# A spectral-and-attention kernel: both halves of a picture in one transfer, eight direct key steps, and a reordered tail

## The chip, the cores and the metric

The kernel runs on one core of one Trainium2 chip. The metric is the device time of one execution in microseconds. The text names the engines as the profile does: PE (TensorE), DVE (VectorE), ACT (ScalarE), POOL (GpSimd) and SP (SyncE). SP, ACT and POOL also issue DMA transfers, each from its own queue, in program order.

## The reference

Four pictures of 64 channels and 96 x 96 pixels pass through two residual layers, each behind a group normalization with 32 groups. The first layer is attention over all 9216 pixels with a sigmoid in place of a softmax, followed by a channel gate. The second multiplies the 16 lowest modes along the width and 32 along the height of a 2-D Fourier transform by complex 64 x 64 matrices.

```python
def reference(x, wq, bq, wk, bk, wv, bv, ca_w1, ca_w2, W_pos_re, W_pos_im, W_neg_re, W_neg_im):
    # layer 0, u = gn(x)
    q, k, v = conv1x1(u)                       # 8, 8 and 64 channels
    att = sigmoid(einsum('bcn,bcm->bnm', Q, K))
    out = einsum('bcm,bnm->bcn', V, att) + u
    scale = sigmoid(mlp(out.mean) + mlp(out.max))
    x = x + out * scale
    # layer 1, u = gn(x)
    u_hat = rfft2(u)
    top = einsum('bchw,cohw->bohw', u_hat[:, :, :16, :16], W_pos)
    bot = einsum('bchw,cohw->bohw', u_hat[:, :, -16:, :16], W_neg)
    return x + irfft2(top and bot put back, zeros elsewhere)
```

## The kernel before

**Layout.** A picture lies in SBUF on 128 partitions of 4608 elements (`HALF`): the upper half of the picture (48 rows of pixels) with its 64 channels on partitions 0 to 63, the lower half on 64 to 127. In DRAM a picture is [64 channels][9216]. `xf` and `outf` are views of it as [half e][channel c][4608]. `read` and `write` (lines 97 to 103) move columns of a picture in two transfers of 64 rows, one for each half, each on a queue that the caller gives. `read` is used for the first loads of all four pictures, for `old` (the original picture, again, for the second layer of the first three), and for `again` (the same for the last one); `write` for the result. The loads of the first picture are nine chunks of 512 columns, with the halves on SP and ACT; the other three are three chunks of 1536 columns each, all on SP. SP also issues the two parts of the constants `cs`, one behind the first picture, one behind the fourth.

**Attention.** Queries go in 9 blocks of 512 (`NBLK`) for each picture. For a block there are 144 tiles of 128 keys by 512 queries; a key step holds eight tiles, so there are 18 steps (0 to 17). A planner ahead of the emission fixes bursts of up to seven tiles: PE makes the energies of burst t+1 (`energies`, L556), ACT their sigmoids (`sigmoids`, L577), and PE multiplies those of the burst before with the values (`attend`, L594). PE, ACT and DVE run in exactly that written order (`manual_schedule`). Other work is put between bursts: `together` beside a burst (in PSUM banks that it leaves free), `alone`, and `ends` behind it.

For the first picture keys are made beside the attention that uses them. A *direct* key step is a matmul into PSUM (`key_matmuls`, L441) and three DVE instructions (`key_splits`: L452, L453, L436) that write `kT`. `DIRECT` is the number of such steps. The others come with the values: `values_of` projects 512 pixels (L475); DVE takes `u` and the values (L492, L482), splits them into high and low parts (L510, L511) and transposes them (L513); SP sends the result to DRAM in `qk` (L517); POOL fetches it into `stage` with the rows repeated (`known_keys`, L526); and DVE copies it into `kT` (L528), two bursts after the fetch was written down for the first picture and six for the others. Queries of later blocks come back from `qk` through SP (`queries`, L534). In block s, `values_of` leaves the key part out while 2s is below `DIRECT`.

**Second layer of the first three pictures.** It runs hidden beside the attention of the next picture, in strips of 768 columns: `fetch` reads `old`, `result` forms the layer's input on DVE (L185) and stores it, `turned`, `along_w` and `along_h` are the transform, `mixing` and `back_h` go back to DRAM and return through `zd` (L384 loads `z` in four transfers for each call), and `back_w` loads the stored input, adds (L403) and writes the result.

**Tail.** The last picture's gate and second layer have nothing to hide behind. Around the gate, matmuls on the constants with no use for the result keep PE busy: two at L923 ahead of it, and `occupy(n, behind, pd, cols)` (L970), which issues n of them behind a given instruction. Then, strip by strip, DVE forms the input (strips 4 and 5 by ACT and an adding DMA of POOL), transposes it (L1001), and PE transforms along W into `pa`, in two groups of three strips (L1011). `rows_turned(n)` transposes one group (L1018); `rows(n)` transforms along H into `pu` (L1023). The statistics go by `steps`: `steps[3]` is the matmul at L170, DVE's `ve` (L172) and POOL's power (L173). The mixing is 256 small matmul records (L220), of which DVE and ACT take turns to move the result out (L135, L137). `keep` stores six of the eight groups of rows in DRAM (`vd`, L231), `back` loads them into `vt` with the modes on partitions (L242): 16 rows in four transfers, and 8 rows in four. The last two groups come by `picked`, a matmul that selects rows, and DVE adds them to `vt` (L1104). Then the inverse along H (`pz_last`, L1114), four transposes (L1122), the inverse along W (`py`, L1132), the addition to the picture (L1140), and the writes (L103) of half a strip twice and five strips.

Of the kernel before, what the change touches and what calls it, by code (L numbers as in the profile page):

```python
# [33 lines left out]
F32 = mybir.dt.float32  # L34
# [6 lines left out]
P = 128  # L41
B, C, H, W = 4, 64, 96, 96
# [5 lines left out]
KW = 16  # L48
# [6 lines left out]


SIZE, HEAD = 7, 4
DIRECT = 12
AHEAD = 6 * SIZE
ALL = B * NBLK * TILES  # L60
ENGINES = {mybir.EngineType.PE, mybir.EngineType.Activation, mybir.EngineType.DVE}
# [23 lines left out]
NGROUP = 2  # L85
NPICK = 2
PICK = C + 4 * (NPICK - 1)
LATE = {"fw": NSQ * P, "fh": NGROUP * 2 * P, "pick": SIDE * PICK, "gh": 2 * P}


@with_exitstack
def tile_kernel(ctx: ExitStack, tc: tile.TileContext, x, cst, late, spec, out):
# [1 line left out]
    xf = x.rearrange("b c (e h) w -> b e c (h w)", e=2)  # L94
    outf = out.rearrange("b c (e h) w -> b e c (h w)", e=2)

    def read(to, p, cols, queues):
        for e in range(2):
            queues[e].dma_start(to[bass.ts(e, C)], xf[p][e, :, cols])

    def write(p, cols, of, queues):
        for e in range(2):
            queues[e].dma_start(outf[p][e, :, cols], of[bass.ts(e, C)])  # L103

    const = ctx.enter_context(tc.tile_pool(name="const", bufs=1))
    xpool = ctx.enter_context(tc.tile_pool(name="xpool", bufs=1))
# [5 lines left out]
    for p in range(B):  # L112
        xt = xpool.tile([P, HALF], F32, tag=f"x{p}", name=f"x{p}")
        step = NB if p == 0 else 3 * NB
        for s in range(HALF // step):
            cols = bass.ts(s, step)
            read(xt[:, cols], p, cols, (nc.sync, nc.scalar if p == 0 else nc.sync))
        if p == 0:
            nc.sync.dma_start(cs[:, :NFIRST], cst[:, :NFIRST])
        xs.append(xt)  # L120
# [4 lines left out]
    def named(name, rows=P):  # L125
        return cs[:rows, PLACE[name]]
# [118 lines left out]
    class Hidden(Mixing):  # L245
# [14 lines left out]
        def fetch(self, p, s):  # L260
            self.olds[p, s] = self.work.tile([P, STRIP], F32, tag="old", bufs=2,
                                             name=f"old_{p}_{s}")
            read(self.olds[p, s], p, bass.ts(s, STRIP), (nc.sync, nc.sync))

        def result(self, p, s, gate):

# [121 lines left out]
        def back_w(self, p, s):  # L388


            cols = bass.ts(s, STRIP)
            old = self.work.tile([P, STRIP], F32, tag="old", bufs=2, name=f"x1_{p}_{s}")
            nc.sync.dma_start(old, self.x1d[p][:, cols])
            py = self.banks(2)
            for i in range(2):
                for r in range(2):
                    rows, at = bass.ts(r, C), bass.ts(r, 2 * W)
                    for e in range(2):
                        nc.tensor.matmul(py[bass.ts(e, C), r, bass.ts(i, 2 * W)],  # L399
                                         self.z[rows, H // 8 * e + 2 * s + i, p, :],  # L400
                                         named("gw")[rows, at], start=True, stop=True)
# [3 lines left out]
            write(p, cols, old, (nc.sync, nc.sync))  # L405

    with tc.tile_pool(name="work", bufs=1) as work, \
# [289 lines left out]
        def bring(s):  # L699

            if s == 0:
                again.append(xpool.tile([P, HALF], F32, tag="vT0", name="again"))
            cols = bass.ts(s, STRIP)
            read(again[0][:, cols], B - 1, cols, (nc.sync, nc.sync))

        chain, ready, started = [], [0], [0]

# [211 lines left out]
        spare[0] = 7  # L919
        gate, steps, f = after(B - 1)  # L920
        with tc.issue_after(attended[0].ins):
            for n in (NB, NB // 2):
                nc.tensor.matmul(banks[:, 3, :n], cs[:, :P], cs[:, :n], start=True, stop=True)  # L923
        for step in steps:
            step()
# [2 lines left out]
    with tc.tile_pool(name="tail", bufs=1, reuse_waits="tile") as tail, \  # L928
# [45 lines left out]
        l1 = Mixing(1, bank_m, evacuate)  # L974
        l1.wts = wts
        idle = small_bank.tile([P, NB], F32, tag="idle", name="idle")
        occupy(3, projected[0], idle)

        mr, steps, mv = group_stats(None, bank_m, "l1_last")
        less = small.tile([P, 1], F32, tag="less", name="less")  # L980
# [54 lines left out]
        with tc.manual_schedule(engines=ENGINES):  # L1035
            for s in range(NSTRIP):
                if s not in ADDED:
                    combine(p, s, gate, again[:, bass.ts(s, STRIP)])
                strip(s)
                if s in (1, 3):  # L1040
                    steps[s // 2]()
            var = small.tile([P, 1], F32, tag="var", name="var")
            rows_turned(0)
            rows(0)
            nc.vector.tensor_reduce(var, squares, AX.X, ALU.add)
            nc.vector.tensor_scalar(mv[:, 1:2], var, 1.0 / HALF, None, ALU.mult)
            steps[2]()
            steps[3]()
            rows_turned(1)
            rows(1)  # L1050
            nc.vector.tensor_scalar(less_constant, mr[:, 0:1], mr[:, 1:2], float(-H),
                                    ALU.mult, ALU.mult)
            nc.vector.transpose(t, pu.rearrange("q (c k) -> q k c", k=KW))
            for h in (slice(0, 8), slice(8, KH)):
                nc.scalar.activation(u[:, :, :, h, 0], turned[:, :, :, h], AF.Copy,
                                     scale=mr[:, 1:2])
                for to, of in ((lo, hi), (hi, lo)):
                    nc.vector.tensor_scalar(
                        u[to, :, :, h, 1], turned[of, :, :, h], mr[of, 1:2],
                        -1.0 if to == lo else 1.0, ALU.mult, ALU.mult)  # L1060
                if h.start == 0:
                    l1.constant_mode(0, less_constant)
# [16 lines left out]
        for q in range(KH // 4):  # L1079
            l1.mix(q, 0)  # L1080
            l1.mix(q, 1)
            if q <= last - NPICK:
                l1.keep(q, nc.sync)
            if q == 3:
                nc.gpsimd.memset(vt, 0.0)
            for first, rows_of, behind in ((0, 16, last - 1), (16, 16 - 4 * NPICK, last)):
                if q == behind:
                    with tc.issue_after(moved[1].ins):
                        for half in range(2):
                            for slot in range(2):  # L1090
# [11 lines left out]
                        picks[:, 2 * half + n, at:at + C], l1.vms[q][:, bass.ts(2 * half + n, M)],  # L1102
                        start=(q == last - NPICK + 1), stop=(q == last))
        nc.vector.tensor_tensor(vt, picked, vt, ALU.add)  # L1104
        occupy(1, l1.last, mix_bank.tile([P, NB], F32, tag="v", name="idle_v", bufs=6), NB // 2)

        banks.close()
        pz_bank, py_bank = psum("ps_z"), psum("ps_y", 2)
        pz = pz_bank.tile([P, 4, NB], F32, tag="z", name="pz_last")
        for i in range(2):  # L1110
            for e in range(2):
                for half in range(2):
                    rows_of = bass.ts(half, 2 * KH)
                    moved[0] = nc.tensor.matmul(  # L1114
                        pz[:, 2 * e + half, :].rearrange("q (k o) -> q k o", o=C)[
                            :, :, bass.ts(i, C // 2)],
                        gh[rows_of, e, :], vt[rows_of, :].rearrange("q (k o) -> q k o", o=C)[
                            :, :, bass.ts(i, C // 2)], start=True, stop=True)
        z = tail.tile([P, C, SQ], F32, tag="z", name="z_last")
        for i in range(4):  # L1120
            cols = bass.ts(i, C // 4)
            nc.vector.transpose(z[:, cols, :],  # L1122
                                pz.rearrange("q x (k o) -> q o (x k)", o=C)[:, cols, :])
        occupy(2, moved[0], py_bank.tile([P, 2, NB], F32, tag="y", name="idle_y")[:, 0])
        for s in range(NSTRIP):
            for part in ([0], [1]) if s == 0 else ([0, 1],):
                py = py_bank.tile([P, 2, NB], F32, tag="y", name=f"py_{s}_{part[0]}")
                for n, i in enumerate(part):
                    for r in range(2):
                        rows_of = bass.ts(r, C)  # L1130
                        for e in range(2):
                            nc.tensor.matmul(  # L1132
                                py[bass.ts(e, C), r, bass.ts(n, 2 * W)],
                                z[rows_of, :, H // 8 * e + 2 * s + i],
                                named("gw")[rows_of, bass.ts(r, 2 * W)], start=True, stop=True)
                n = len(part)
                cols = slice(s * STRIP + part[0] * STRIP // 2,
                             s * STRIP + (part[0] + n) * STRIP // 2)
                o = x1[:, cols].rearrange("q (i r m) -> q i r m", r=2, m=2 * W)
                nc.vector.tensor_tensor(  # L1140
                    o, py[:, :, :2 * W * n].rearrange("q r (i m) -> q i r m", i=n), o, ALU.add)
                write(p, cols, x1[:, cols], (nc.sync, nc.scalar))


def _constants(l0):
# [68 lines left out]
    fours = np.zeros((2 * KH, 2, 4, SQ))  # L1214
    fours[..., :H // 4] = np.concatenate(gh, 1).reshape(2 * KH, 2, H // 4, 4).transpose(0, 1, 3, 2)
    b.append(np.tile(fours.reshape(2 * KH, 2 * P), (2, 1)))
    return a, np.concatenate(b, 1).astype(np.float32)


# [28 lines left out]
```

## Time and profile before

| what | us |
|---|---|
| median of 3 runs (lowest, highest) | 3045.09 (3043.98, 3045.64) |
| the profiled execution | 3046.73 |
| its span, from the first to the last instruction | 3044.6 |
| PE busy | 3012.3 |
| ACT busy | 2406.3 |
| DVE busy | 338.1 |
| POOL busy | 135.2 |

The span leaves out what the device spends before the first and after the last instruction of the kernel, 2.1 us of the profiled execution. Busy times are sums over instructions; PE's end times are modelled, so a busy PE is not one at its peak. The granted clock of PE is 0.996 over the span. The page of the profile lists DMA queue 1 (SP), 10 (ACT) and 0 (POOL); a DMA packet is one row of a transfer, and some packets of four bytes come with each transfer beside its rows.

### The profile page before, as it was taken

What the parts mean: (1) busy time and instruction counts of PE and PEld (TensorE: products, weight loads), DVE (VectorE), ACT (ScalarE), POOL (GpSimd) and SP (SyncE); (2) the same over time, 40 slices, a digit from 0 to 9 for tenths busy, and PEclk for the clock granted to TensorE, in tenths of its full rate; (3) what the DMA queues carried; (4) which work ended last, traced back from release to release, by engine and by line L of the source; (5) the groups of instructions that cost most, each with busy time, mean ns of one, the idle gap of its engine ahead of it and who ended that gap; (6) DMA issues with size and microseconds to landing.
All of it is one profiled execution on the core that took longest, in us unless ns stands there. A gap on an engine that the chain in (4) does not pass through costs nothing.

```text
span 3044.6 us, 44711 instructions
## 1 busy us (share of the span) xinstructions
PE 3012.3 (99%) x19368; PEld 1097.0 (36%) x19368; DVE 338.1 (11%) x818; ACT 2406.3 (79%) x1539; POOL 135.2 (4%) x275
## 2 busy tenths in 40 slices
PE   7999999999999999999999999999999999999997
PEld 3333333333333333333333333333333333333334
DVE  3200000002211000001311000000221100000004
ACT  4788888887888888888788888888788777777782
POOL 0100000003100000001300000000310000000000
PEclk9999999999999999999999999999999999999999
DMA  6100000002230000000332000000244243312224
GB/s 153 23 4 4 4 4 4 4 1 46 75 80 17 4 4 4 4 4 21 73 78 72 4 4 4 4 4 2 44 108 98 91 141 88 53 51 69 60 85 152
DMA packets 156869, 133.00 MB, mean 44 GB/s; under 512 B 118752, under 2 KB 123040, under 8 KB 156384
## 3 DMA queue, kind: packets, MB, share of 16 engines
q1 hardware_dynamic: 144544, 108.85, 14.2%
q0 software_dynamic: 10704, 18.83, 2.1%
q8 instruction: 152, 2.49, 0.3%
q10 hardware_dynamic: 1424, 2.46, 0.3%
q14 instruction: 45, 0.37, 0.0%
HBM read 90.81 MB, written 38.47 MB: 42 GB/s over the span
## 4 chain that ended last, share of the span: by engine, by line
PE 97%; DMA 1%; issue 0%; DVE 0%; ACT 0%; SPq 0%; ACTq 0%; POOL 0%; DVEq 0%
PE banks L594 77%; PE banks L556 16%; DMA x<-in_x_dram 1%; PE banks L475 1%; PE banks L220 1%; PE banks L399 0%; PE pv L220 0%; PE banks L305 0%; ACT at L577 0%; PE pa L1011 0%; PE banks L371 0%; DMA qk<-turned 0%; PE banks L333 0%; PE idle L970 0%; PE banks L441 0%
## 5 line engine op out<-in xcount | busy, mean ns | idle before, releaser
L577 ACT ACTIVATE at<-banks 128x2048 f32<-128x2048 f32 (+1 forms) x1505 | 2388.6, 1638 | 563.9 <-PE banks L556 545.1
L594 PE MATMUL banks<-at,vT 128*64 128x512 f32 (+1 forms) x11780 | 2410.6, 549 | 0.0
L594 PEld LDWEIGHTS banks<-at,vT 128*64 128x64 f32 x11780 | 774.3, 136 | 1352.3 <-issue 1297.5
L556 PE MATMUL banks<-q,kT 32*128 32x512 f32 x5040 | 543.3, 453 | 0.6 <-ACT at L577 0.4
L556 PEld LDWEIGHTS banks<-q,kT 32*128 32x128 f32 x5040 | 224.0, 183 | 453.4 <-issue 330.1
L600 DVE SCALAR_TENSOR_TENSOR x<-banks,x 128x512 f32<-128x512 f32 x36 | 24.9, 691 | 1664.9 <-PE banks L594 1664.9
L526 POOL DMA_DIRECT2D stage<-qk x240 | 117.9, 499 | 959.1 <-DMA qk<-turned 951.4
L173 POOL TENSOR_TENSOR mr_l<-ve_l,cs 128x1 f32<-128x1 f32 x7 | 3.9, 556 | 1292.4 <-DVE ve_l L172 1292.4
L403 DVE TENSOR_TENSOR x<-banks,x 128x768 f32<-128x768 f32 x18 | 17.2, 958 | 212.5 <-PE banks L399 201.4
L475 PEld LDWEIGHTS banks<-cs,x 64*64 64x64 f32 x1152 | 22.8, 136 | 27.3 <-ACT at L577 25.3
L492 DVE TENSOR_TENSOR u<-banks,cs 128x128 f32<-128x128 f32 x35 | 10.2, 290 | 189.8 <-PE banks L475 189.8
L744 POOL DMA_DIRECT2D w_early<-in_spec_dram x12 | 6.4, 543 | 521.7 <-PE banks L399 357.5
L475 PE MATMUL banks<-cs,x 64*64 64x80 f32 (+1 forms) x1152 | 28.5, 237 | 0.0
L556 PE MATMUL banks<-q_first,kT 32*128 32x512 f32 x144 | 18.0, 463 | 9.8 <-DVE full_k L452 6.6
L482 DVE TENSOR_TENSOR vT<-banks,cs 128x256 f32<-128x256 f32 x72 | 26.9, 414 | 0.0
L720 DVE COPY ae<-banks 128x512 f32<-128x512 f32 x9 | 6.2, 692 | 174.8 <-PE banks L305 128.9
L602 DVE TENSOR_REDUCE maxs<-x 128x1 f32<-128x512 f32 x36 | 24.7, 686 | 1.2
L608 DVE BATCH_NORM_STATS2 stats<-x 128x6 f32<-128x512 f32 x36 | 23.4, 680 | 6.1 <-DMA x<-in_x_dram 6.0
L720 DVE COPY ws<-banks 128x512 f32<-128x512 f32 x16 | 11.1, 691 | 116.8 <-PE banks L220 116.8
L185 DVE SCALAR_TENSOR_TENSOR x<-x,gate,old 128x768 f32<-128x768 f32 x18 | 18.2, 1009 | 17.7 <-DMA old<-in_x_dram 17.7
L513 DVE STREAM_TRANSPOSE turned<-t 128x384 f32<-128x384 f32 (+1 forms) x35 | 19.2, 549 | 1.2
L273 DVE STREAM_TRANSPOSE old<-x 128x768 f32<-128x768 f32 x18 | 17.6, 978 | 0.6
(143 smaller groups left out, 411.8 us busy)
## 6 DMA issues: line engine op xcount, KB each, us to landing
ws<-in_spec_dram SPq DMA_DIRECT2D x32, 512.0 KB
q<-qk SPq DMA_DIRECT2D x280, 32.0 KB
out_dram<-x SPq DMA_DIRECT2D x41, 192.0 KB
stage<-qk POOLq DMA_DIRECT2D x240, 32.0 KB, 1.9
x<-in_x_dram SPq DMA_DIRECT2D x18, 384.0 KB
old<-in_x_dram SPq DMA_DIRECT2D x36, 192.0 KB
x1d<-x SPq DMA_DIRECT2D x18, 384.0 KB
xd<-old SPq DMA_DIRECT2D x18, 384.0 KB
```

The costliest lines, as they stand in the source:

```text
L185: nc.vector.scalar_tensor_tensor(xs[p][:, cols], xs[p][:, cols], gate, old, ALU.mult, ALU.add)
L220: self.last = nc.tensor.matmul(pv[bass.ts(g, 32), :].rearrange("q (n k o) -> q n k o", n=SIDE, o=C)[:, :, k, :], self.ut[:, at:at + 32], s ...
L475: projected[0] = nc.tensor.matmul(pp[bass.ts(e, P // 2), b, 2 * a + h, :width], src[rows, a, h, bass.ts(e, P // 2)], named("wv")[rows, :wi ...
L482: nc.vector.tensor_tensor(vTs[p % 2][:, 8 * s:8 * s + 8, :].rearrange("p (a h b) m -> p b a h m", h=2, b=2)[:, b], pp[:, b, :, :C].rearran ...
L513: nc.vector.transpose(turned[:, k:].rearrange("p k a (m h) -> p (k a) h m", h=2), t[:, k:].rearrange("p k a h m -> p (k a) h m").bitcast(F32))
L526: nc.gpsimd.dma_start(come[bass.ts(r, QK), :], split[p][s // 2][:, r // 2, bass.ts(s % 2, NB // 2)])
L556: nc.tensor.matmul(banks[:, bank_of(i), :], kT[r:r + 32, i % TILES // 8, i // 4 % 2, :], ask[i // TILES][r:r + 32, :], start=True, stop=True)
L577: nc.scalar.activation(at[:, of:of + n, :], banks[:, bank:bank + n, :], AF.Sigmoid)
L594: attended[0] = nc.tensor.matmul(acc[half, cols], vTs[n // NBLK % 2][:, j, :], at[:, place(2 * pair + b), cols], start=(j == 0), stop=(j = ...
L600: nc.vector.scalar_tensor_tensor(blk, acc, 1.0, blk, ALU.mult, ALU.add, accum_out=sums[p][:, m:m + 1])
L602: mark[0] = nc.vector.tensor_reduce(maxs[p][:, m:m + 1], blk, AX.X, ALU.max)
L608: each = [lambda s=s: nc.vector.bn_stats(stats[:, s, :], xs[p][:, bass.ts(s, NB)]) for s in range(NBLK)]
```

## The change

- `read` and `write` issue one transfer for both halves. Its side in SBUF has 128 partitions; its side in DRAM has the dimensions [2 halves][64 channels][columns]. All reads go by SP. Writes in the tail go by SP and ACT in turn, a whole transfer each.
- `DIRECT` is 8 instead of 12: key steps 8 to 11 of the first picture now come through `qk` and `stage`.
- In the gate the fillers of L923 are 512, 512 and 128 columns instead of 512 and 256; the three fillers of 512 columns on `idle` become one of 512 and one of 256, and stand behind the two on `pa`.
- `rows_turned(1)` stands ahead of `steps[3]`.
- The loads into `vt` are no longer tied to ACT's last copy. The first 16 rows are issued by POOL, written down at q = 4, the next 8 by SP, at q = 5.
- `pz_last` becomes two tiles of half the channels, each transposed behind its own matmuls; the filler ahead of it is 512 columns instead of 256; the constants `gw` for the last inverse come with `late`, in another order of rows.

```diff
-DIRECT = 12
+DIRECT = 8
...
-LATE = {"fw": NSQ * P, "fh": NGROUP * 2 * P, "pick": SIDE * PICK, "gh": 2 * P}
+LATE = {"fw": NSQ * P, "fh": NGROUP * 2 * P, "pick": SIDE * PICK, "gh": 2 * P, "gw": 4 * W}
...
-    def read(to, p, cols, queues):
-        for e in range(2):
-            queues[e].dma_start(to[bass.ts(e, C)], xf[p][e, :, cols])
-
-    def write(p, cols, of, queues):
-        for e in range(2):
-            queues[e].dma_start(outf[p][e, :, cols], of[bass.ts(e, C)])
+    def read(to, p, cols, queue):
+        queue.dma_start(to, xf[p][:, :, cols])
+
+    def write(p, cols, of, queue):
+        queue.dma_start(outf[p][:, :, cols], of)
...
-            read(xt[:, cols], p, cols, (nc.sync, nc.scalar if p == 0 else nc.sync))
+            read(xt[:, cols], p, cols, nc.sync)
...
-            for n in (NB, NB // 2):
+            for n in (NB, NB, NB // 4):
                 nc.tensor.matmul(banks[:, 3, :n], cs[:, :P], cs[:, :n], start=True, stop=True)
...
-        occupy(3, projected[0], idle)
...
             with tc.issue_after(projected[0].ins):
-                nc.tensor.matmul(along_w[n][:, 3 * NB // 2:], cs[:, :P], cs[:, :NB // 2],
-                                 start=True, stop=True)
+                filled = nc.tensor.matmul(along_w[n][:, 3 * NB // 2:], cs[:, :P], cs[:, :NB // 2],
+                                          start=True, stop=True)
+        occupy(1, filled, idle)
+        occupy(1, filled, idle, NB // 2)
...
             steps[2]()
+            rows_turned(1)
             steps[3]()
-            rows_turned(1)
             rows(1)
...
-            for first, rows_of, behind in ((0, 16, last - 1), (16, 16 - 4 * NPICK, last)):
+            for first, rows_of, behind, queue in ((0, 16, last - 3, nc.gpsimd),
+                                                  (16, 16 - 4 * NPICK, last - 2, nc.sync)):
                 if q == behind:
-                    with tc.issue_after(moved[1].ins):
-                        for half in range(2):
-                            for slot in range(2):
-                                l1.back(vt, 64 * half + 32 * slot, first, rows_of, 0, slot,
-                                        2 * half, 2, (nc.scalar, nc.sync)[slot])
+                    for half in range(2):
+                        for slot in range(2):
+                            l1.back(vt, 64 * half + 32 * slot, first, rows_of, 0, slot,
+                                    2 * half, 2, queue)
...
-        occupy(1, l1.last, mix_bank.tile([P, NB], F32, tag="v", name="idle_v", bufs=6), NB // 2)
+        occupy(1, l1.last, mix_bank.tile([P, NB], F32, tag="v", name="idle_v", bufs=6))
...
-        pz = pz_bank.tile([P, 4, NB], F32, tag="z", name="pz_last")
+        z = tail.tile([P, C, SQ], F32, tag="z", name="z_last")
         for i in range(2):
+            pz = pz_bank.tile([P, 4, NB // 2], F32, tag=f"z{i}", name=f"pz_{i}")
             for e in range(2):
                 for half in range(2):
                     rows_of = bass.ts(half, 2 * KH)
                     moved[0] = nc.tensor.matmul(
-                        pz[:, 2 * e + half, :].rearrange("q (k o) -> q k o", o=C)[
-                            :, :, bass.ts(i, C // 2)],
-                        gh[rows_of, e, :], vt[rows_of, :].rearrange("q (k o) -> q k o", o=C)[
-                            :, :, bass.ts(i, C // 2)], start=True, stop=True)
-        z = tail.tile([P, C, SQ], F32, tag="z", name="z_last")
-        for i in range(4):
-            cols = bass.ts(i, C // 4)
-            nc.vector.transpose(z[:, cols, :],
-                                pz.rearrange("q x (k o) -> q o (x k)", o=C)[:, cols, :])
+                        pz[:, 2 * half + e, :], gh[rows_of, e, :],
+                        vt[rows_of, :].rearrange("q (k o) -> q k o", o=C)[:, :, bass.ts(i, C // 2)],
+                        start=True, stop=True)
+            for n in range(2):
+                cols = slice(i * C // 2 + n * C // 4, i * C // 2 + (n + 1) * C // 4)
+                nc.vector.transpose(z[:, cols, :], pz.rearrange(
+                    "q x (k o) -> q o (x k)", o=C // 2)[:, bass.ts(n, C // 4), :])
...
-                                named("gw")[rows_of, bass.ts(r, 2 * W)], start=True, stop=True)
+                                parts["gw"][rows_of, bass.ts(r, 2 * W)], start=True, stop=True)
...
-                write(p, cols, x1[:, cols], (nc.sync, nc.scalar))
+                write(p, cols, x1[:, cols], (nc.sync, nc.scalar)[(s + part[0]) % 2])
```

The other calls of `read` and `write` give SP's queue alone, as before. The scheduler sets `old` for the first two strips of the second layer early in SP's queue, before and after: nothing holds them back.

More of the change, by code (lines that the diff above doesn't have):

```diff
@@ L262, in fetch @@
                                              name=f"old_{p}_{s}")
-            read(self.olds[p, s], p, bass.ts(s, STRIP), (nc.sync, nc.sync))
+            read(self.olds[p, s], p, bass.ts(s, STRIP), nc.sync)
         def result(self, p, s, gate):
@@ L404, in back_w @@
                 o, py[:, :, :4 * W].rearrange("p r (i m) -> p i r m", i=2), o, ALU.add)
-            write(p, cols, old, (nc.sync, nc.sync))
+            write(p, cols, old, nc.sync)
     with tc.tile_pool(name="work", bufs=1) as work, \
@@ L703, in bring @@
             cols = bass.ts(s, STRIP)
-            read(again[0][:, cols], B - 1, cols, (nc.sync, nc.sync))
+            read(again[0][:, cols], B - 1, cols, nc.sync)
         chain, ready, started = [], [0], [0]
@@ L1216, in _constants @@
     b.append(np.tile(fours.reshape(2 * KH, 2 * P), (2, 1)))
+    by_half = np.arange(2 * KW).reshape(2, 2, KW // 2).transpose(1, 0, 2).ravel()
+    b.append(np.kron(np.eye(4), np.concatenate([twice * cw.T, -twice * sw.T], 0)[by_half]))
     return a, np.concatenate(b, 1).astype(np.float32)
```

## The prediction

> **What bounds the kernel now.** I read the page first: its busy shares, then the chain that ended last. The span is matmul throughput nearly everywhere.
>
> ```profile
> span 3044.6 us, 44711 instructions
> PE 3012.3 (99%) x19368; PEld 1097.0 (36%) x19368; DVE 338.1 (11%) x818; ACT 2406.3 (79%) x1539; POOL 135.2 (4%) x275
> ```
>
> PE is idle for only 32 us, so a change outside the attention loop gains at most that and what fillers take in the tail. It can lose far more: PE is in order, and it stops when keys are late. So the start comes next, in the chain of waits from 0 to 140 us (start, duration, what):
>
> ```profile
> 2.27 4.62 DMA x<-in_x_dram
> 6.91 4.00 DMA x<-in_x_dram
> ...
> 13.52 12.79 DMA x<-in_x_dram
> 26.33 14.79 DMA x<-in_x_dram
> 41.13 5.73 DMA qk<-turned
> ```
>
> All four pictures are loaded by 41 us, and until then the small transfers of queries and keys stand behind them on SP's queue. That costs one PE stall of 6.6 us. From the timeline of 40 to 130 us:
>
> ```profile
> 47.58 0.79 PE L556 MATMUL banks<-q_first,kT 32*128 32x512 f32 x1 [6.56 <-DVE full_k L452]
> ...
> 75.93 0.73 PE L556 MATMUL banks<-q_first,kT 32*128 32x512 f32 x7
> ...
> 92.20 4.14 POOL L526 DMA_DIRECT2D stage<-qk  x8 [75.17 <-DMA qk<-turned]
> ```
>
> The first burst of energies has 5 tiles, later ones 7; counting bursts, the one at 75.93 holds tiles 61 to 67, so the energy of tile 64, the first that needs key step 8 (8 tiles a step), runs at 76.0 us. The direct steps are 0 to 11 now, and the first keys that come back from DRAM arrive at 96 to 98 us, in time.
>
> Then the DMA side, in stretches (share of 16 DMA engines and GB/s are the last two columns):
>
> ```profile
> 33.00:41.00 8.00, 8.00 (x102) 3.58 (x101) 3.20 (x10) 3.79 (x3) 0.00 (x0) 1.00 1.02 234
> 2904.00:2914.00 10.00, 10.00 (x61) 3.38 (x57) 0.00 (x0) 9.04 (x6) 2.65 (x5) 1.00 1.02 409
> 3025.40:3029.20 3.80, 3.72 (x17) 3.31 (x18) 0.02 (x1) 0.00 (x0) 0.00 (x0) 0.55 0.00 0
> ```
>
> With 64 rows at a time the picture loads reach 234 GB/s with all 16 engines busy; 128-row weights reach 409, or 25.6 bytes a ns for each engine. In the tail (third line) the matmuls of pz run at a granted clock of 0.55.
>
> **How many engines a transfer gets.** The DMA view of 2622.9 to 2630 us holds just four ws<-zd transfers (L384), each of 8 outer by 24 inner rows:
>
> ```profile
> DMA  0003245576775665766566656676666655523310
> ...
> DMA packets 800, 0.39 MB, mean 55 GB/s; under 512 B 32, under 2 KB 800, under 8 KB 800
> ```
>
> The data are 4 x 192 = 768 packets, so 32 are left, 8 for each transfer, and the share stands at 5 to 7 tenths. A transfer of 64 rows leaves 16: ACT's nine x loads make 720 = 9 x (64 + 16) packets in the first 60 us. I read the small packets as one for each engine that takes part (the slices agree: 8 of 16 busy), so 192 rows behind an outer dimension of 8 had 8 engines, not 16. The changed transfers have two halves outermost in DRAM.
>
> [...] By it every read and write of a picture runs on two engines, and the sum is a large loss. [...] no row here shows an outer 2. [...]
>
> **The change part by part.** The sum is made against the profiled execution (3046.7 us, of which 2.1 lie around the span); it is 1.6 above the median of the runs, 3045.1.
>
> *Loads on two engines.* Each of the two moves half of each picture: 4 x 64 rows x 18,432 B = 4.72 MB, at 25.6 B/ns 184 us. From 2.1 us that is 186, and their eight rows each of the two constants transfers (2452 + 3472 B) add 2: 188. The rate is unknown for two engines alone; the nearest bounds are 25.6 and 234/16 = 14.6. I take the upper, since two engines ask for 51 GB/s of a path that gives 234; the lower would put the loads at 325 us.
>
> *Eight direct steps.* Step 8 now goes u, turned (L513), qk (SP), stage (POOL), kT (DVE). On SP's queue the qk transfers stand behind all loads, and a share of each lies on the two slow engines. After 188: the end of the second qk set, q_1, the third set, q_1 again: 13 issues of 0.42 us and one landing of 2, 195.5. Next in SP's order stand two old loads for the second layer, which nothing holds back so early: 2 x 64 x 3072 B / 25.6 = 15.4 us on the two engines, 211. Then qk of block 4 (0.9, and 1.2 to land) 213; four stage issues of 0.5 (499 ns on the page) and 1.9 to land, 217; the copy (0.24), 217.4. PE would be at tile 64 by about 107 us, although the last chunk of picture 0 comes 38 us later (nine chunks of 64 x 2048 B / 25.6 take 46 us, not 9): 76 + 38 less the old stall. So PE waits from there to 217.4, against 76.0 before: **+141.4**. ACT and DVE queue behind the same wait (the kT copy stands ahead of u of block 6). Keys 9 to 17 then follow at 2 us each and are wanted at 3.8 to 4.6: nothing. Four key steps leave PE; three of them lay after tile 64: 3 x 0.63 = **-1.9**. The removed stall of 6.6 us is inside the difference.
>
> *Old, again and out in the second layer.* Each old or out takes 7.7 us plus landing, where it took about 2. Old is covered by the 23 us between strips (six bursts of 3.8, which is 0.66 of L556 and 3.16 of L594 in the chain), except where DVE already waited 6.75 us for it (third strip of each hidden picture); there 5 us more, under attention that needs DVE only at block ends. The outs of the first three pictures come every 12 us and SP has 3 us of q loads in 80: covered; if not, back_w would hold a bank. I put **+3** for all.
>
> *The gate and along-W.* Gate fillers go from 768 to 1152 columns, 2.3 us for 1.56: they end at 2982.4, when f arrives: 0, costing their excess if f were earlier. Behind the gate 1280 filler columns stand ahead of pa in place of 2048; L970's 1536 took 4.54 us at a low clock. PE lags the strips there, so pa ends about 1.4 earlier. The row turn of group 1 (L1018, 1.24) moves ahead of ve (L172): it no longer waits for pv, while ve and POOL's pow wait for it, but both are done 1 us before pu. rows(1) follows at once instead of 1.4 after: together the mixing starts **-2.9** earlier.
>
> *Modes back.* The vt loads stood behind ACT's last copy (3018.5) and landed at 3024.5. Now 16 rows go by POOL once q 0 to 3 have landed (4 x 0.5 + 1.9, beside the mixing) and 8 rows by SP behind the last vd (3017.0, landing 1.8; four issues of 0.3, landing 1.5): 3021.6. The sum into vt starts **-3.0**. No POOL work waits behind its loads.
>
> *pz and z.* A filler of 512 columns leaves PE 1 us idle, not 4.2, so the clock should hold; two tiles let the first two transposes (0.63 each) run beside the second half. 3.7 + 2.5 becomes about 3.5: **-2.7**. The wider late constants (904 KB for 712) cost 0.5 us at 409 GB/s 70 us before use: 0. The py loop is the same.
>
> *Last writes.* The first out issues at 3033.0 - 8.6 = 3024.4, moves from 3025.5 (1.1 later, as before), and each of the two engines has 64 x 18,432 B = 1.18 MB: 46.1 us, from both queues alike. With 1.4 of landing the end is 3073.0 for 3044.6: **+28.4**, the 8.6 gained in it.
>
> Sum: 141.4 - 1.9 + 3 + 28.4 = +171: 3216 us as a median of runs.
>
> **The rivals.**
> A. *All 16 engines serve the single transfer, and it is faster.* [...] Against: the 32 packets. Loads end at 27 us instead of 41, the 6.6 stall goes, the first chunks come 2.9 earlier, four key steps save 2.5, the tail 8.6: -20.6, 3024. It decides from about eight engines up: then 9.4 MB at 8 x 25.6 end before 50 us and step 8 is there for its tile.
> B. *Two engines, and slower than bytes alone.* If two engines reach only about 20 B/ns, loads end at 240 and the writes take 59: about 3285. The same if old, twice as late at the third strips, stops PE through DVE.
> C. *It cancels.* With six engines the loads would end at 63 us and step 8 would come some 12 us late, against 11 gained in the tail and by fewer steps: within 0.2%. [...]
>
> **How the numbers follow.** The likeliest case 0.81 at 3216, its own range 3195 to 3245; B 0.08; A 0.09; C 0.02. The range 3190 to 3275 leaves out A, C and the far part of B. About 0.2% (6 us) is what a measurement of this kernel can tell from no change. Faster 0.09, same 0.02, slower 0.89.
>
> **What would show it.** Right: four-byte packets fall to 2 for a picture transfer, the DMA share between 5 and 185 us is near 2/16 at about 50 GB/s, one PE stall of over 80 us ends with kT<-stage at 210 to 225, the mixing starts some 21 us after the gate, and the last write ends some 45 us after the last DVE addition. Wrong: DMA slices of 9 and 350 GB/s or more at the start (A); a stall without end near 217 (another queue or rate); PE gaps near the strips of the second layer (B).

## The result and the profile after

The changed kernel takes 3225.7 us (median of four runs, 3224.7 to 3227.3) against 3045.3 beside it: 1.0594 times as long, 95% interval 1.0575 to 1.0612. The profiled execution took 3225.3 us, its span 3223.5.

The page of the changed kernel shows that the matmul work is the same and that PE now stands idle for about 207 us of it, where it was 32:

```profile
span 3223.5 us, 44581 instructions
PE 3016.3 (94%) x19360; PEld 1096.4 (34%) x19360; DVE 336.0 (10%) x814; ACT 2406.8 (75%) x1539; POOL 145.2 (5%) x295
```

The stretches of the changed kernel's start (busy time of PE, PEld, DVE, ACT and POOL, then PE's clock, the share of 16 DMA engines and GB/s) show the transfers at two sixteenths, 0.125, and a little more from what else moves, where the kernel before had all sixteen busy (1.02 from 33 to 41 us):

```profile
2.00:50.00 48.00, 9.77 (x16) 4.00 (x16) 5.55 (x8) 0.23 (x2) 0.00 (x0) 1.00 0.15 54
50.00:188.00 138.00, 28.61 (x228) 14.90 (x228) 12.54 (x36) 16.02 (x13) 0.56 (x1) 0.60 0.14 56
```

In the trace's packets a row of 6144 bytes takes 238 ns here and 422 ns in the kernel before: each of the two engines is faster than one of sixteen (25.8 bytes a ns against 14.6), but there are only two. The last such row of the loads starts at 186.9 us.

On SP's timeline (start, duration, instruction) the small transfers of queries and keys (L515, L532) follow the loads. The issues of the loads take long themselves. Five of the last nine take 14.6 to 14.8 us each, near the 15.2 that each of the two engines needs for its 64 rows at 238 ns: SP is held at the pace of the transfers.

```profile
42.20 111.33 SPq L98 DMA_DIRECT2D x<-in_x_dram  x9
153.58 14.72 SPq L119 DMA_DIRECT2D cs<-in_cst_dram  x1
168.42 20.60 SPq L515 DMA_DIRECT2D qk<-turned  x8
```

PE's timeline has one long stall, and it is not the one that was forecast. It ends with full_k after 30 energy tiles. Tile 64, which needs the first key from DRAM, waits only 2.85 us more:

```profile
190.09 0.79 PE L554 MATMUL banks<-q_first,kT 32*128 32x512 f32 x1 [108.01 <-DVE full_k L450]
...
220.19 0.51 PE L554 MATMUL banks<-q_first,kT 32*128 32x512 f32 x4 [2.85 <-DVE kT L526]
```

What DVE waited for there stands in its own timeline, and the same wait stands among the waits of the kernel before (total, times, longest):

```profile
189.55 0.48 DVE L450 TENSOR_SCALAR full_k<-banks,cs 128x256 f32<-128x256 f32 x1 [112.04 <-DMA qk<-turned]
```

```profile
DVE full_k L452 <- DMA qk<-turned: 10.6, 1, 10.6
```

A direct key step writes full_k into a buffer of tag "turned". There are two of these, shared with the turned queries and keys that SP writes to DRAM (qk). Until such a write has landed the buffer isn't free, and the write stood behind the loads in SP's queue.

At the other end, the DMA view of the changed kernel from 3194 us to the end shows two engines working alone, with PE, ACT and DVE done (the last addition ends at 3180.2):

```profile
DMA  1111111111111111111111111111111111111100
...
DMA packets 488, 1.47 MB, mean 50 GB/s; under 512 B 10, under 2 KB 10, under 8 KB 488
...
q10 hardware_dynamic: 354, 1.07, 8.9%
q1 hardware_dynamic: 134, 0.40, 3.3%
```

Here both ACT's queue (q10) and SP's (q1) have writes under way, and together they still reach 50 GB/s, with shares that add up to 12.2% of sixteen engines, or 1.95 engines: the second queue brought no others in.

### The profile page after: what moved, and what is told of

The parts are those of the page before. It is cut to its first block, busy times and chain, and to the rows that moved or that the text cites. A ratio compares the mean times of both kernels' runs of the same rounds, so it can differ in the third digit from the quotient of the medians.

```text
span 3223.5 us, 44581 instructions
## 1 busy us (share of the span) xinstructions
PE 3016.3 (94%) x19360; PEld 1096.4 (34%) x19360; DVE 336.0 (10%) x814; ACT 2406.8 (75%) x1539; POOL 145.2 (5%) x295
## 4 chain that ended last, share of the span: by engine, by line
PE 89%; SPq 6%; DMA 2%; DVE 1%; issue 0%; ACT 0%; POOL 0%; DVEq 0%; POOLq 0%; ACTq 0%
PE banks L592 71%; PE banks L554 15%; SPq L98 5%; DMA qk<-turned 1%; PE banks L473 1%; SPq L515 1%; PE banks L218 0%; SPq L119 0%; PE banks L397 0%; DMA xd<-old 0%; DMA old<-in_x_dram 0%; PE pv L218 0%; PE banks L303 0%; SPq L117 0%; PE banks L369 0%
## 5 line engine op out<-in xcount | busy, mean ns | idle before, releaser
L524 POOL DMA_DIRECT2D stage<-qk x256 | 125.8, 499 | 1081.8 <-DMA qk<-turned 1070.3
L650 PE MATMUL banks<-x 128*128 128x256 f32 (+1 forms) x30 | 16.6, 679 | 41.2 <-DMA x<-in_x_dram 41.2
L554 PEld LDWEIGHTS banks<-q_first,kT 32*128 32x128 f32 x144 | 8.0, 193 | 127.2 <-DVE full_k L450 108.3
L650 PEld LDWEIGHTS banks<-x 128*128 128x128 f32 x30 | 8.0, 311 | 48.1 <-DMA x<-in_x_dram 47.0
```

Source lines behind the costliest of these rows:

```text
L524: nc.gpsimd.dma_start(come[bass.ts(r, QK), :], split[p][s // 2][:, r // 2, bass.ts(s % 2, NB // 2)])
L554: nc.tensor.matmul(banks[:, bank_of(i), :], kT[r:r + 32, i % TILES // 8, i // 4 % 2, :], ask[i // TILES][r:r + 32, :], start=True, stop=True)
L650: nc.tensor.matmul(banks[:, 7, :n], xs[0][:, s * NB:s * NB + P], xs[0][:, s * NB:s * NB + n], start=True, stop=True)
```

## The experiments

Times are medians; the kernel before, run beside them, was at 3046.1 to 3046.3 us. "Tile 64" is the start of the energy of that tile.

**Undo the transfers, keep everything else.** Line numbers are those of the kernel before here.

```diff
-    def read(to, p, cols, queue):
-        queue.dma_start(to, xf[p][:, :, cols])
+    def read(to, p, cols, queues):
+        for e in range(2):
+            queues[e].dma_start(to[bass.ts(e, C)], xf[p][e, :, cols])
...
```

> The changed kernel with every picture transfer issued as two of 64 rows again, on the queues of before (SP and ACT for picture 0 and the last writes, SP twice elsewhere); eight direct key steps and all edits of the tail stay. Theory (the single transfer is the whole loss): no stall of over 10 us, and the shortenings measured in the changed kernel's trace stay: gate to mixing -2.4, mixing to the vt sum -2.6, vt sum to the first py addition -2.3, and up to -2.5 for four key steps: 3035 to 3038 us. Rival (eight direct steps cost by themselves): the keys of step 8 come back from DRAM at some 96 us as step 12's did before, but are wanted at 76: a PE stall of about 20 us at tile 64 and 3055 us or so.

Measured: 3036.75 us (3033.76 to 3037.24), ratio 0.9967 (0.9955 to 0.9980). The single transfer is the whole loss, and the other edits gain 9.4. Against this kernel's trace the loss of the changed one splits into start, middle and tail: tile 64 from 74.5 to 220.2 us (+145.7), tile 64 to the gate's fillers from 2902.0 to 2908.4 (+6.4), fillers to the end from 58.5 to 94.9 (+36.4). The sum, 188.5, is the difference of the spans. The rival fails: key step 8 is not late with loads on all engines. PE's one stall is full_k's, as it was before the change:

```profile
48.03 0.79 PE L556 MATMUL banks<-q_first,kT 32*128 32x512 f32 x1 [6.30 <-DVE full_k L452]
```

**The transfers alone.** The kernel before with the changed read and write; in the last writes the two queues alternate. DIRECT stays at 12.

```diff
-    def read(to, p, cols, queues):
-        for e in range(2):
-            queues[e].dma_start(to[bass.ts(e, C)], xf[p][e, :, cols])
+    def read(to, p, cols, queue):
+        queue.dma_start(to, xf[p][:, :, cols])
...
```

> The kernel before with the single transfer alone (SP for the reads and hidden writes, the last writes alternating between SP and ACT); twelve direct steps and the old tail stay. Theory (the stall is full_k's wait for the shared buffer at tile 34, which the number of direct steps does not touch): the same stall of about 108 us ended by DVE full_k; start +144, last writes +38, the middle +2 to +4, none of the shortenings: 3229 to 3235 us. Rival (the prediction's: PE waits for the first keys from DRAM): the first such keys are step 12's, 32 tiles or some 18 us of PE work later, so the start loses only about 125: 3208 to 3216 us, with kT<-stage at the end of the long wait.

Measured: 3238.2 us (3236.1 to 3239.4), 3 us above the theory's range, 22 above the rival's. The start loses 149.4 us (tile 64 at 225.4, although it needs no key from DRAM here), the stretch from there to the gate's fillers 6.6. The PE waits of this kernel (total, times, longest) name the shared buffer, with twelve direct steps as with eight:

```profile
PE banks L554 <- DVE full_k L450: 107.5, 1, 107.5
PE banks L554 <- DVE kT L434: 3.3, 1, 3.3
```

**full_k out of the shared buffer.**

```diff
-            u = qp.tile(shape, F32, tag="turned", name=f"full_k_{p}_{s}")
+            u = stage[:, s % NSTAGE, :]
```

> The changed kernel, but full_k of the direct key steps lies in a free slot of stage (slot s of 8, which the returning keys fill only from step 8 on) and not in the two buffers that it shares with turned. Theory: the wait of 108 us at tile 34 goes, and the next one takes its place: PE runs on to tile 64 at some 110 to 120 us and waits there for kT<-stage until 215 to 225. Time within 5 us of the changed kernel's 3225.7. Rival (the shared buffer is the cause by itself): nothing is late next, and the time falls by most of 108, to 3120 to 3150 us.

Measured: 3228.0 us (3226.3 to 3229.8). The time is the theory's, the place is not: PE stops after 40 tiles, not 64. The waits of DVE and PE in this kernel:

```profile
DVE turned L511 <- DMA qk<-turned: 107.3, 1, 107.3
...
PE banks L554 <- DVE kT L434: 100.3, 1, 100.3
...
PE banks L554 <- DVE kT L526: 10.3, 1, 10.3
```

Now turned itself (L511) is the third writer of its two buffers; it stands ahead of a direct key's last step (L434) in DVE's written order. Only then comes the wait for the first key from DRAM (L526), 10.3 us.

**All 18 key steps of picture 0 direct, on top of that.**

```diff
-DIRECT = 8
+DIRECT = 18
```

> As e3_own_buffer, with all 18 key steps of picture 0 direct, so that none of its keys comes back from DRAM. Theory (the small qk transfers stand behind all loads on SP's queue, and whatever needs them first waits): the next to be late are the queries of block 1 at tile 144, which PE reaches at some 160 us and which land near 195: a stall of 30 to 40 us instead of about 105, ten more key steps at 0.6 us each, so 3155 to 3175 us. Rival (PE starves for picture 0 itself or for anything else on the two engines, not for keys): still 3210 us or more.

Measured: 3219.9 us, 45 above the theory's range: a miss, by the same step. No key of picture 0 comes from DRAM any more, but its queries do, through turned. DVE's wait is there again:

```profile
DVE turned L511 <- DMA qk<-turned: 109.5, 1, 109.5
```

So the number of direct steps is not what costs the time. Whatever DVE executes behind a turned tile waits for the writes in SP's queue.

**The qk writes of picture 0 on POOL, the single transfers kept.**

```diff
-                    nc.sync.dma_start(
+                    (nc.gpsimd if p == 0 else nc.sync).dma_start(
                         split[p][s][:, k:].rearrange("r k (a g m) -> g r (k a) m", a=2, g=4)[g],
```

> The changed kernel, with the qk writes of picture 0 issued by POOL instead of SP. Theory (what is late is what SP issues behind its paced loads, not data on busy engines): DVE's wait for qk<-turned falls below 5 us and the stall of 108 us goes; PE keeps the 40 us by which the chunks of picture 0 come later, and waits next for the queries of block 1, which SP still issues behind the loads at 169 us and which are wanted at tile 144, near 160: 10 to 15 us. Start about +50 instead of +144: 3125 to 3140 us. Rival (the two busy engines hold the small transfers whatever queue issues them): the keys stay late, 3200 us or more.

Measured: 3159.5 us (3158.2 to 3160.8). The stall of 108 us is gone and tile 64 runs at 105.5: the transfers were late for standing behind SP's loads, not for busy engines. The size is missed by 20 us. PE's next wait is the one named, the queries of block 1:

```profile
197.58 0.76 PE L554 MATMUL banks<-q,kT 32*128 32x512 f32 x1 [24.41 <-DMA q<-qk]
```

SP comes to these queries at 176.65, not 169, and their eight issues take 20.7 us (3.8 for eight of another block later in the changed kernel). The waits for keys and values between tile 64 and there, 1.0 to 5.2 us each, are 13 us more.

**The first loads and the last writes on POOL's queue.** The question is whether this shape gets more than two engines when POOL issues it.

```diff
-            read(xt[:, cols], p, cols, nc.sync)
+            read(xt[:, cols], p, cols, nc.gpsimd)
...
-                write(p, cols, x1[:, cols], (nc.sync, nc.scalar)[(s + part[0]) % 2])
+                write(p, cols, x1[:, cols], nc.gpsimd)
```

> The changed kernel, with the single transfers of the four first loads and of the last writes issued by POOL; old, again and the hidden outs stay on SP. Theory [...] loads end at 30 to 50 us, the last writes take some 10 to 15 us: 3036 to 3060 us. Rival (two fixed engines for this shape from any queue): 3200 us or more.

Measured: 3090.8 us (3084.3 to 3091.7): far nearer to the theory, but 31 above its range. The DMA view of 2 to 50 us shows that more than two engines work (the first row is the busy share by slice, in tenths):

```profile
DMA  8955669999999851115224533567989999979999
...
DMA packets 9797, 7.14 MB, mean 149 GB/s; under 512 B 8200, under 2 KB 8200, under 8 KB 9797
...
q0 software_dynamic: 9265, 5.63, 69.7%
```

POOL's packets alone fill 69.7% of the time of sixteen engines, as much as 11 of them, where all transfers of the changed kernel have a share of 0.15 in the same stretch. The trace doesn't name the engine of a packet, so how POOL's transfers come to more engines is not shown. Still, 149 GB/s are under the 234 of 64-row transfers, 8200 of the packets are small, and the last row of the loads ends at 79.3 us, not at 30 to 50. The profiled run is the fastest of the four (3084.3). In it the first energies come at 56.5 us for 21.0 in e1_two_halves, tile 64 at 103.7 (+29), the middle costs 5.9 (its old, again and out are still single transfers on SP), and the tail 12.5.

**Twelve direct steps with two halves.** In e1_two_halves:

```diff
-DIRECT = 8
+DIRECT = 12
```

> e1_two_halves with twelve direct steps. Theory (four key steps of 0.63 us are all that the number changes where nothing stalls): 2 to 3 us above e1_two_halves' 3036.8, 3038.5 to 3040. Rival (the keys that return from DRAM cost PE as much in another place): equal to e1_two_halves.

Measured: 3039.6 us, 2.8 above e1_two_halves, as the theory said, although the runs of the two overlap (3036.4 to 3042.0 and 3033.8 to 3037.2).

**Two halves, and the qk writes of picture 0 on POOL.** In e1_two_halves:

```diff
-                    nc.sync.dma_start(
+                    (nc.gpsimd if p == 0 else nc.sync).dma_start(
```

> e1_two_halves with the qk writes of picture 0 on POOL. Theory (its last stall, 6.3 us ended by DVE full_k, is the same wait for the shared buffer behind the loads on SP): the stall goes and the time falls by 5 to 6.5 to 3030.5 to 3032 us, under both kernels. Rival (the first qk writes would wait for data or engines anyway, or the stall moves to another PE wait): within 2 us of e1_two_halves' 3036.8.

Measured: 3029.31 us (3028.6 to 3031.4), ratio 0.9946 (0.9933 to 0.9960): 16.9 us below the kernel before, and 1.2 below the theory's range. Tile 64 moves from 74.5 to 67.1. The stall of 6.3 us is 0.84 here:

```profile
40.97 0.50 PE L556 MATMUL banks<-q_first,kT 32*128 32x512 f32 x1 [0.84 <-DVE full_k L452]
```

The wait that cost 108 us in the changed kernel was thus there before it, with 6.6, and it goes when the small writes leave the queue of the loads. Half clock falls on 3.41 us of this start, where e1_two_halves has 6.83 and 10.24 us of it, and that is part of the gain. This is the fastest kernel of the study. The next four kernels change one thing in it; in their traces, too, full_k stops PE for 0.8 to 0.9 us, and tile 64 runs at 66.6 to 70.4.

**Only the last writes single.** Here write_whole is the changed kernel's write.

```diff
-                write(p, cols, x1[:, cols], (nc.sync, nc.scalar))
+                write_whole(p, cols, x1[:, cols], (nc.sync, nc.scalar)[(s + part[0]) % 2])
```

> e8_two_halves_qk_pool with the last writes alone as single transfers, alternating between SP and ACT. Theory (the last writes are bytes over two engines whatever the start was, and nothing of it overlaps with the start's loss): 37 to 39 us above e8_two_halves_qk_pool's 3029.3, 3066 to 3069 us, the end some 45 us or more after the last addition. Rival (part of the changed kernel's long tail came from elsewhere): under 3060 us.

Measured: 3066.8 us (two runs, 3064.1 and 3069.5): 37.5 more. The end is 43.6 us behind the last addition, for the 45 expected. Nothing covers the tail, and it adds to the start in full.

**Only old, again and out single.**

```diff
-            read(self.olds[p, s], p, bass.ts(s, STRIP), (nc.sync, nc.sync))
+            read_whole(self.olds[p, s], p, bass.ts(s, STRIP), nc.sync)
...
-            read(again[0][:, cols], B - 1, cols, (nc.sync, nc.sync))
+            read_whole(again[0][:, cols], B - 1, cols, nc.sync)
...
-            write(p, cols, old, (nc.sync, nc.sync))
+            write_whole(p, cols, old, nc.sync)
```

> e8_two_halves_qk_pool with the single transfer only for old, again and out while the attention runs. Theory (the slow again and old transfers hold up xT behind them on SP, at one place, the fourth picture's along-H step, where the changed kernel lost 5.5 us against e1_two_halves): 5 to 6.5 above e8_two_halves_qk_pool's 3029.3, 3034.5 to 3036 us, with one PE wait of 2 to 4 us for xT<-xd. Rival (the prediction's +3, spread over DVE's waits for old): 3031 to 3033 us with no such PE wait.

Measured: 3037.4 us, 8.1 more (3035.4 to 3045.8). The place is right, the size 1.6 too small. PE waits once for xT, and its clock is then low:

```profile
2285.73 1.92 PE L311 MATMUL banks<-xT,cs 96*32 96x512 f32 x4 [3.06 <-DMA xT<-xd]
2287.58 5.00 PE L600 MATMUL banks<-at,vT 128*64 128x256 f32 x16
```

```profile
2285.25:2292.00 6.75, 6.27 (x18) 1.79 (x20) 0.69 (x1) 1.02 (x1) 0.00 (x0) 0.50 0.18 66
```

The trace's clock records have half clock here for 6.83 us. PE is busy in 6.27 us of the stretch, which loses about 3.1 us beside the wait of 3.06, and the two are 6.2 of the 7.2 us by which the energies fall further behind those of e8_two_halves_qk_pool around this place. Another 2.2 arise near 80 us.

**The loads of vt as before.**

```diff
-            for first, rows_of, behind, queue in ((0, 16, last - 3, nc.gpsimd),
-                                                  (16, 16 - 4 * NPICK, last - 2, nc.sync)):
+            for first, rows_of, behind in ((0, 16, last - 1), (16, 16 - 4 * NPICK, last)):
                 if q == behind:
+                    with tc.issue_after(moved[1].ins):
...
-                                    2 * half, 2, queue)
+                                        2 * half, 2, (nc.scalar, nc.sync)[slot])
```

> e8_two_halves_qk_pool with the loads of vt as before (ACT and SP, behind ACT's last copy). Theory: the vt sum comes 2.5 to 3 later after the mixing, PE is idle 3.5 to 4 us ahead of pz instead of 1.1, its clock falls and pz takes up to 1.5 longer: 3032 to 3034 us. Rival (another path sets the vt sum, the picks or vd): within 1 us of 3029.3.

Measured: 3032.2 us (3031.8 to 3033.0), 2.9 more. The loads of modes on other queues are worth that. In the trace the sum into vt comes 1.9 us later behind the start of the mixing than in e8_two_halves_qk_pool. After 3.06 us of idleness pz took 2.58 us for 2.17, and the half clock lasts on behind it: from the sum to the first addition it is 6.98 us for 5.44, the 1.5 that was allowed for.

**256 columns of filler ahead of pz.**

```diff
-        occupy(1, l1.last, mix_bank.tile([P, NB], F32, tag="v", name="idle_v", bufs=6))
+        occupy(1, l1.last, mix_bank.tile([P, NB], F32, tag="v", name="idle_v", bufs=6), NB // 2)
```

> e8_two_halves_qk_pool with 256 columns of filler ahead of pz instead of 512. Theory (an idle stretch of under some 2 us, as ahead of e1_two_halves' pz, is not long enough to lower the clock): pz takes 2.2 us as there, the time is within 1 us of 3029.3. Rival (the filler holds the clock): the granted clock in pz falls to about 0.55 as before the change, pz takes 3.7 us, 3030.5 to 3031.5 us.

Measured: 3030.3 us (3027.9 to 3034.3), not to be told from 3029.3. In the one trace, that of the slowest of the five runs, pz behaves as the rival said. Timelines of PE, first of this kernel, then of e11_old_vt:

```profile
3013.01 3.86 PE L1116 MATMUL pz<-vt,lc 64*128 64x256 f32 x16 [1.75 <-DVE vt L1105]
```

```profile
3011.78 2.58 PE L1116 MATMUL pz<-vt,lc 64*128 64x256 f32 x16 [3.06 <-DVE vt L1105]
```

The shorter idle stretch has the slower pz. The clock records tell why: both kernels have one stretch at half clock, of 3.41 us by the records, here from 3013.26 and in e11_old_vt from 3013.20. In the stretches of this kernel and then of that one the clock is 0.50 alike:

```profile
3013.25:3016.60 3.35, 3.35 (x16) 2.80 (x15) 1.31 (x2) 0.00 (x0) 0.00 (x0) 0.50 0.00 0
```

```profile
3013.25:3016.60 3.35, 3.35 (x9) 1.55 (x6) 2.40 (x4) 0.00 (x0) 0.00 (x0) 0.50 0.00 0
```

Here all but the first 0.25 us of pz lies in it; there pz was over half done when it began, and what follows pz pays. From the sum into vt to the first addition the two take 7.12 and 6.98 us, for 5.44 in e8_two_halves_qk_pool, so the stretch costs 1.5 to 1.7 us in both. The other four runs have no trace, and whether they had it is not known. A filler is judged on several runs: this kernel's times spread over 6.4 us, e8_two_halves_qk_pool's over 2.8.

## Why the prediction was right, and where it was not

The forecast was 3216 us, slower; measured were 3225.7. In the two profiled executions:

| Step | Forecast | Measured |
|---|---|---|
| Start, up to tile 64 | +141.4 | +144.2 (76.0 to 220.2) |
| Tile 64 to the gate's fillers | +1.1 | +4.3 (2904.1 to 2908.4) |
| Gate to mixing | -2.9 | -2.4 |
| Mixing to the sum into vt | -3.0 | -2.6 |
| That sum to the first py addition | -2.7 | -2.3 |
| First addition to the end | +37.0 | +37.8 (12.2 to 49.9) |
| Sum | +171 | +178.9 |

*Two engines.* Right, with the rate. The loads were to end at 188, and their last row of 6144 bytes starts at 186.9. The seven last writes leave 14 packets of four bytes, two each, as forecast for two engines. Two packets of 2048 bytes or more are under way at once for 172 of the first 187 us. Rival A, all sixteen engines, would have had 0.9 or more as the DMA share; it was 0.14. What carried over is the reading of the small packets, 8 for a transfer with 8 outermost and here 2 with 2; the 409 GB/s of the 128-row weights did not. Why the count of engines goes with that dimension was not shown. Rival B's rate fails too: each engine reached 25.8 bytes a ns, not 20. Its other part, a stop of PE through DVE, came true on a small scale (below, the middle). C fails with A.

*Who waits at the start.* The failed step is "Step 8 now goes u, turned (L513), qk (SP), stage (POOL), kT (DVE)", with "PE waits from there to 217.4". The chain of transfers behind the loads was right, and so tile 64 ran at 220.2. But PE was not standing there: it had stopped 138 us earlier, after 30 tiles, for full_k. The prediction read the 6.6 us stall of before as gone ("the removed stall of 6.6 us is inside the difference"), when it was this very wait, and grew to 108. e3_own_buffer shows that the wait doesn't hang on full_k alone: with this holder of the two buffers removed, turned stops DVE itself, and the time stays within 3 us. That the total still fits is in part luck. The keys of step 8 came at 219.8, behind old as forecast; but PE, released at 190.1 with 34 tiles to do, was at tile 64 only at 217.3. So the wait left out and the one counted end within 3 us of each other, and in e2_only_single the start loses 149.4 us without the one counted. The count of direct steps, which the prediction made part of the loss, costs nothing: e7_two_halves_12 has the four steps as a gain of 2.8, and e1_two_halves, with eight, has no late key.

*The middle.* The term "I put **+3** for all" was mis-sized. Against e1_two_halves the single transfers cost 6.4 there, and the three key steps gained 2.1 (2904.1 to 2902.0), near the 1.9 forecast. What failed is that old is "covered", "under attention that needs DVE only at block ends". In the timelines of the changed kernel DVE waits 16.46 us for old at the third strip of the last hidden picture, where 5 more than the 6.75 of before were forecast; SP's store of the strip (L270) waits for DVE, the loads of xT (L281) stand behind it in SP's order, and PE waits for xT:

```profile
2431.45 1.02 DVE L183 SCALAR_TENSOR_TENSOR x<-x,gate,old 128x768 f32<-128x768 f32 x1 [16.46 <-DMA old<-in_x_dram]
```

```profile
2432.50 0.33 SPq L270 DMA_DIRECT2D x1d<-x  x1
2432.87 2.15 SPq L281 DMA_DIRECT2D xT<-xd  x3
```

```profile
2437.90 1.05 PE L303 MATMUL banks<-xT,cs 96*32 96x512 f32 x4 [2.74 <-DMA xT<-xd]
```

e10_hidden_whole has the same chain, with 19.65 us of DVE and 3.06 of PE. The half clock after it (3.41 and 6.83 us) was not named either.

*The tail.* Each term came within 0.8 us. That the clock would hold in pz was right: 1.00 in the changed kernel for 0.55. "A filler of 512 columns leaves PE 1 us idle, not 4.2, so the clock should hold" was right for the changed kernel, but 1.69 us idle kept it in e1_two_halves while 1.75 lost it in e12_short_filler: the idle time alone does not decide (the last section has more). Of the 9.4 us that the edits other than the transfers gain, e7_two_halves_12 gives 2.8 to the direct steps and e11_old_vt 2.9 to the loads of vt; the edits of the gate, rows_turned and the two tiles of pz were not run alone. Between gate and mixing the kernel before has 3.41 us at half clock from 2984.44, and the changed one has none.

## What to carry to other kernels

Ahead of merging two transfers into one, look at the outermost dimension on the DRAM side: 2 there left two of sixteen engines, 50 GB/s for 234, and a second hardware queue didn't help. When a queue gets slower, look for every buffer whose release hangs on a transfer in that queue, not only for its data, and follow short waits of the profile before to their end: PE's 6.6 us were ended by DVE, DVE's own 10.6 by a DMA write, and this is the wait that grew to 108. Such a wait may also be had back: moving the small writes off the queue of the loads gained 7.4 us on top of the other edits, a part of it by the clock.

## What had not been expected of the hardware

- Issuing held the engines that issued, at the pace of the transfers. In the changed kernel nine issues of loads took SP 111.3 us, five of them 14.6 to 14.8 each, and four last writes held ACT for 27.1 us, after its work was done. What held them is not shown.
- Two engines alone moved 25.8 bytes a ns each, by packets of 6144 bytes; sixteen together on 64-row transfers, in the kernel before, 14.6 each.
- Every stretch at half clock in the clock records of the kernel before and of the changed one, but for the first and last of a run, lasts 3.41 us or a multiple of it (3.41 and 10.24 before, 3.41, 6.83 and 112.64 after).
- How busy PE was went with the clock that followed. The stretches at full clock between them are multiples of 3.41 us too (13.65 and 2928.64 before), so these two traces were cut into pieces of that length at the records' edges. Of 1755 pieces at full clock, all seven in which PE was busy for less than 0.43 were followed by half clock, and none of the 1746 above 0.61; of the two between, at 0.59 and 0.60, one was. All eight returns to full clock came behind a piece of 0.97 or more. In the 3.41 us ahead of their half clock in pz, PE was busy for 0.42 in e11_old_vt and 0.49 in e12_short_filler. PE's ends are modelled, so the bounds are rough, and they are those of these two traces.
- The waits of 2.74 us (changed kernel) and 3.06 us (e10_hidden_whole) for xT inside the attention went, with the half clock behind them, with a loss of 5.5 and 7.2 us.
